# Transposing a 4096 x 4096 adjacency: by DMA from a bf16 copy in DRAM, in place of TensorE's products with the identity

## The chip, the cores and the metric

The kernel runs on one core of a Trainium2 chip. The metric is the time of one execution on the device, in microseconds, as the median of several runs. A profile is one further execution with the hardware profiler on.

## What is computed

The input is x (4096 nodes x 512) and a 0/1 adjacency of 4096 x 4096 in float32. Two graph layers follow each other, each with a residual and a layer normalisation:

```python
# layer 0: graph attention, 4 heads of 128
support = (x @ weight).reshape(N, 4, 128)
logits  = f1[j] + f2[i]              # of support, per head
w       = leaky_relu(logits, 0.2) * adjacency[i, j]
attn    = softmax over j of w where it is not 0
out     = attn @ support + bias + x @ proj_w + proj_b
x1      = layernorm(x + out)
# layer 1: masked attention, 8 heads of 64
adj     = max(adjacency, eye)
scores  = q @ k.T / 8 + 0.01 * eye - 1e16 * (1 - adj)
out     = layernorm(x1 + softmax(scores) @ v @ Wo)
```

Both layers sum over the neighbours j of a node i, and both put j on the partitions, since the products over j contract along the partitions. So both need the adjacency with j on the partitions and i along the free dimension, which is the transpose of the order in which it lies in DRAM.

## The kernel before, in words

The function is `tile_gat_then_masked_attention` (from line 430). The order of the instructions on each engine is that of the program text, so where a call stands decides what waits behind it in a queue. The stages:

1. **Layer-0 projections** (lines 569 to 675, 0 to 285 us). Eight groups g of 512 rows, four tiles of 128 rows each. TensorE transposes x (line 634) and multiplies by the two weights (lines 647 and 651); VectorE makes f1 and f2, GpSimd scales support (line 606), SP stores base (line 667), support (line 611) and the row factors (line 619) to DRAM.
2. **Layer-0 attention** (lines 683 to 802, 316 to 1314 us). Four windows w of 1024 nodes i, four heads h in each, 32 blocks j of 128 neighbours: 512 steps. A step makes z on ScalarE (line 712), masks it with the transposed adjacency on VectorE (line 715, one for two steps), forms p (line 719), and eight products on TensorE add into o_ps (line 793). `front` runs LA = 3 steps ahead of the products. After a window's last head, ScalarE divides, GpSimd adds base by an accumulating DMA (line 752), and the normalised rows are stored (line 762) and transposed for layer 1.
3. **Layer-1 projections** (lines 808 to 858): q, k and v to DRAM.
4. **Layer-1 attention** (lines 860 to 1067, from 1693 us). Eight groups g of 512 nodes, four pairs of heads m, 32 blocks j: 1024 units, three to a step. Scores on TensorE (line 933), exponential on ScalarE (line 942), mask on VectorE (line 948), sums on GpSimd (line 956), products on TensorE (line 966). The four blocks on the diagonal use md, a float32 copy of their part of the adjacency to which VectorE adds the diagonal (line 889). `loads` (line 901) fetches k and v one chunk of eight units ahead, the next group's adjacency during m = 3, and md during m = 1.

**The adjacency's way.** `load_rows` (line 536) has GpSimd load 1024 rows x 512 columns from DRAM and narrow them to bf16 on the way, into one of two buffers `arow`. `transpose_adj` (line 543) makes eight 128 x 128 transposes of one block j of a window (line 553, into PSUM), ScalarE copies them to `stage` (line 560), and SP stores two blocks at a time to the DRAM tensor `adjT_d` (line 562). Window 0 is made during the layer-0 projections, one block per tile of 128 rows and two more; windows 1 to 3 during layer-0 attention of the window before, one block every third step while u = 32h + j is below 96. `load_adjT0` (line 565) loads a tile of 128 x 4 x 1024 bf16 (1 MB) of it for layer 0, into 9 buffers of which a window uses 8; the loads of the next window are issued during head 3. In layer 1, `load_adjT` (line 876) loads 128 x 8 x 512 (1 MB) and `load_md` (line 880) has GpSimd load 128 x 4 x 512 and widen it to float32 on the way.

Of the kernel before, what the change touches and what calls it, by code (L numbers as in the profile page):

```python
# [429 lines left out]
def tile_gat_then_masked_attention(  # L430
# [46 lines left out]
    ident_b = const.tile([P, P], BF16, name="ident_b")  # L477
    make_identity(nc, ident_b)
# [19 lines left out]
    adjT_d = [dram.tile([P, NT, W], BF16, name=f"adjT_d{w}") for w in range(NW)]  # L498
# [28 lines left out]
    with tc.tile_pool(name="l0", bufs=1) as l0, \  # L527
            tc.tile_pool(name="l0a", bufs=2) as rows_p, \
# [5 lines left out]
        arow, stage, adjT = {}, {}, {}  # L534

        def load_rows(w, c):
            arow[w, c] = rows_p.tile([P, WT, CJ * P], BF16, name="arow")
            nc.gpsimd.dma_start(  # L538
                arow[w, c],
                adj[w * W:(w + 1) * W, c * CJ * P:(c + 1) * CJ * P].rearrange(  # L540
                    "(t p) n -> p t n", p=P))

        def transpose_adj(w, j, ps):


            c = j // CJ
            if j % CJ == 0:
                nxt = (w, c + 1) if c + 1 < NCJ else (w + 1, 0)
                if nxt[0] < NW:
                    load_rows(*nxt)  # L550
            p = ps.tile([P, WT, P], BF16, name="at_ps", bufs=1)
            for t in range(WT):
                nc.tensor.transpose(p[:, t, :], arow[w, c][:, t, j % CJ * P:(j % CJ + 1) * P],  # L553
                                    ident_b)

            def go():
                if j % 2 == 0:
                    stage[w, j // 2] = rows_p.tile([P, 2, W], BF16, name="stage")
                s = stage[w, j // 2]
                nc.scalar.activation(s[:, j % 2, :], p.rearrange("p t r -> p (t r)"), AF.Copy)  # L560
                if j % 2:
                    nc.sync.dma_start(adjT_d[w][:, j - 1:j + 1, :], s)
            return go

        def load_adjT0(w, c):
            adjT[w, c] = adjT_p.tile([P, CJ, W], BF16, name="adjT")
            nc.sync.dma_start(adjT[w, c], adjT_d[w][:, c * CJ:(c + 1) * CJ, :])

        with tc.tile_pool(name="l0s", bufs=2) as sp, \
# [19 lines left out]
            load_rows(0, 0)  # L589
# [34 lines left out]
            blocks = list(range(NT))  # L624
            loaded = 0
            for g in range(NG):
# [56 lines left out]
        with tc.tile_pool(name="l0w", bufs=2) as wp, \  # L683
# [16 lines left out]
            def front(w, h, j):  # L700
                n = w * H0 + h
                if n == 0 and j == 0:
                    load_pass(w, h)
                if j == 2 * LA and n + 1 < len(passes):
                    load_pass(*passes[n + 1])
                if h == H0 - 1 and w + 1 < NW and j % CJ == 2:
                    load_adjT0(w + 1, j // CJ)
                fr = fr_t[w, h]
                if j % 2 == 0:
                    z = wp.tile([P, 2, W], BF16, name="z")  # L710
                    for k in range(2):
                        nc.scalar.activation(z[:, k, :], fr[:, 0, :], AF.Abs,  # L712
                                             bias=f1s[:, j + k, h:h + 1], scale=BIG)
                    az = wp.tile([P, 2, W], BF16, name="az")
                    nc.vector.tensor_tensor(az, adjT[w, j // CJ][:, j % CJ:j % CJ + 2, :], z,  # L715
                                            op=ALU.min)
                    az_t[w, h, j // 2] = az
                p = wp.tile([P, W], F32, name="p", bufs=LA + 1)
                nc.vector.scalar_tensor_tensor(p, fr[:, 1, :], dj[:, j, h:h + 1],  # L719
                                               az_t[w, h, j // 2][:, j % 2, :],  # L720
                                               op0=ALU.max, op1=ALU.mult)
                p_t[w, h, j] = p
# [57 lines left out]
            for n, (w, h, j) in enumerate(steps):  # L780
# [16 lines left out]
                if take:  # L797
                    later.at(2, take)
# [6 lines left out]
    with tc.tile_pool(name="l1", bufs=1) as l1:  # L805
# [54 lines left out]
        with tc.tile_pool(name="l1w", bufs=2) as wp, \  # L860
# [11 lines left out]
            def of_group(g, j0, j1):  # L872
                r = g * G % W
                return adjT_d[g * G // W][:, j0:j1, r:r + G]

            def load_adjT(g, c):
                at[g, c] = wp.tile([P, CH, G], BF16, name="adjT1", bufs=NCH + 2)
                nc.sync.dma_start(at[g, c], of_group(g, c * CH, (c + 1) * CH))

            def load_md(g):  # L880

                md = wp.tile([P, GT, G], F32, name="md")
                nc.gpsimd.dma_start(md, of_group(g, g * GT, (g + 1) * GT))  # L883
                mdt[g] = md
# [236 lines left out]
```

## Time and profile before

| | |
|---|---|
| median of three runs | 3914.03 us (3912.95 to 3914.14) |
| profiled execution's own time | 3914.05 us |
| its span | 3912.2 us |
| mean granted TensorE clock | 0.985 |
| TensorE busy | 3780.8 us, 97% |
| VectorE busy | 2536.0 us, 65% |
| GpSimd busy | 2055.2 us, 53% |
| ScalarE busy | 1858.0 us, 47% |
| DMA, mean of the 16 engines | 447.47 MB, 114 GB/s |

The span runs from the first to the last instruction; 1.85 us of the profiled execution lie outside it. A group's row gives the source line, the engine, what it writes and reads, the shape and count, and after the bar its busy time and the mean duration of one in ns, then the idle time of the engine just before these instructions and what ended most of it. A float32 product counts as two instructions on TensorE. Slices are fortieths of the span, 98 us each. SPq, POOLq and ACTq are the queues from which SyncE, GpSimd and ScalarE issue DMAs.

### The profile page before, as it was taken

The page shows a single profiled execution, that of the slowest core. Times are in us where ns is not written, and L with a number is a line of the kernel's source. Part 1 is how long each engine was busy: PE and PEld are TensorE (multiplying, and loading weights), DVE is VectorE, ACT ScalarE, POOL GpSimd, SP SyncE. Part 2 cuts the span into 40 slices and gives each one's busy share as a digit, 9 for nine tenths or more (in the row PEclk, how much of TensorE's full clock was granted, in tenths as well). Part 3 has the DMA queues.
Part 4 walks back from the last instruction along what each step waited for, and adds up shares of the span by engine and source line. Part 5 has one row for each costly group of instructions (what it writes and reads, how often), then busy time and mean ns, then how long its engine had stood idle before and what let it go on. Part 6 is the DMA issues. An engine that isn't in the chain of part 4 may idle for free. (4 is left out here: it accounts for less than half of the span.)

```text
span 3912.2 us, 51842 instructions
## 1 busy us (share of the span) xinstructions
PE 3780.8 (97%) x20490; PEld 1971.1 (50%) x20490; DVE 2536.0 (65%) x2432; ACT 1858.0 (47%) x2113; POOL 2055.2 (53%) x1211
## 2 busy tenths in 40 slices
PE   7987999999999699989999999999999999999998
PEld 3447999999999544433333333333333333333332
DVE  3447999999999400036666666666666666666665
ACT  1226767777666300034554444444444444444443
POOL 2320013030030200048888888888888888888886
PEclk9998999999999799999999999999999999999999
DMA  6885657666430422342322322323223223223211
GB/s 163 195 197 151 148 195 174 193 175 155 171 95 34 135 100 89 108 145 76 116 81 77 112 87 70 116 81 106 91 81 122 64 87 113 89 86 103 78 63 51
DMA packets 232429, 447.47 MB, mean 114 GB/s; under 512 B 21744, under 2 KB 136688, under 8 KB 225008
## 3 DMA queue, kind: packets, MB, share of 16 engines
q1 hardware_dynamic: 179264, 386.38, 29.9%
q0 software_dynamic: 42432, 51.39, 8.0%
q10 hardware_dynamic: 10480, 6.29, 0.5%
q8 instruction: 163, 2.67, 0.3%
q14 instruction: 90, 0.74, 0.1%
HBM read 372.51 MB, written 100.86 MB: 121 GB/s over the span
## 5 line engine op out<-in xcount | busy, mean ns | idle before, releaser
L956 POOL TENSOR_TENSOR q_sum<-q_sum,p 128x1024 f32<-128x1024 f32 x704 | 1660.1, 2358 | 331.7 <-DVE p L948 286.3
L948 DVE TENSOR_TENSOR p<-s_ps,adjT 128x1024 f32<-128x1024 f32 x896 | 1044.4, 1218 | 685.6 <-ACT s_ps L942 668.8
L942 ACT ACTIVATE s_ps<-s_ps 128x1024 f32<-128x1024 f32 x1024 | 971.2, 1008 | 1002.3 <-PE s_ps L933 1001.9
L933 PE MATMUL s_ps<-q_sb,k_sb 64*128 64x512 f32 x4096 | 980.9, 610 | 16.4 <-issue 10.1
L793 PE MATMUL o_ps<-sup_t,p 128*128 128x129 f32 x8192 | 951.6, 277 | 37.9 <-DVE p L719 37.8
L966 PE MATMUL o_ps<-p,v_sb 128*64 128x512 f32 x4096 | 956.3, 601 | 0.0
L793 PEld LDWEIGHTS o_ps<-sup_t,p 128*128 128x128 f32 x8192 | 929.7, 192 | 46.1 <-issue 29.4
L933 PEld LDWEIGHTS s_ps<-q_sb,k_sb 64*128 64x128 f32 x4096 | 367.1, 187 | 627.9 <-issue 388.7
L719 DVE SCALAR_TENSOR_TENSOR p<-fr_t,dj,az 128x1024 f32<-128x1024 f32 x512 | 638.8, 1282 | 34.1 <-PE o_ps L793 6.7
L712 ACT ACTIVATE z<-fr_t,f1s 128x1024 bf16<-128x1024 f32 x512 | 556.2, 1141 | 144.7 <-DVE az L715 118.4
L966 PEld LDWEIGHTS o_ps<-p,v_sb 128*64 128x64 f32 x4096 | 263.0, 136 | 649.9 <-issue 621.5
L715 DVE TENSOR_TENSOR az<-adjT,z 128x2048 bf16<-128x2048 bf16 x256 | 311.7, 1218 | 26.6 <-ACT z L712 26.5
L752 POOL DMA_DIRECT2D agg<-base_d x32 | 29.3, 1046 | 447.8 <-ACT agg L740 446.6
L538 POOL DMA_DIRECT2D arow<-in_adj_dram x32 | 29.9, 933 | 423.1 <-PE at_ps L553 423.1
L560 ACT ACTIVATE stage<-at_ps 128x1024 bf16<-128x1024 bf16 x128 | 130.9, 1023 | 199.8 <-PE at_ps L553 195.5
L948 DVE TENSOR_TENSOR p<-s_ps,md 128x1024 f32<-128x1024 f32 x128 | 150.5, 1218 | 94.6 <-ACT s_ps L942 93.4
L883 POOL DMA_DIRECT2D md<-adjT_d x8 | 6.6, 825 | 353.0 <-DMA v_d<-vg 352.7
L837 DVE COPY kg<-k_ps 128x512 f32<-128x512 f32 x32 | 22.1, 691 | 194.7 <-PE k_ps L834 194.7
L977 PE MATMUL sm_ps<-p,ones 128*32 128x512 f32 x1024 | 136.4, 605 | 0.0
L844 ACT ACTIVATE qg<-q_ps 128x512 f32<-128x512 f32 x32 | 19.1, 598 | 236.3 <-PE q_ps L841 236.3
L661 DVE TENSOR_TENSOR prod<-sup,uv 128x512 f32<-128x512 f32 x64 | 51.8, 809 | 116.7 <-ACT sup L657 116.7
L834 PE MATMUL k_ps<-xT,wk 128*128 128x512 f32 x256 | 116.9, 600 | 10.4 <-DMA xT<-x1T_d 10.4
(89 smaller groups left out, 2111.3 us busy)
## 6 DMA issues: line engine op xcount, KB each, us to landing
adjT<-adjT_d SPq DMA_DIRECT2D x64, 1024.0 KB, 7.5
k_sb<-k_d SPq DMA_DIRECT2D x128, 512.0 KB, 3.5
v_sb<-v_d SPq DMA_DIRECT2D x128, 512.0 KB, 3.5
sup_t<-sup_d SPq DMA_DIRECT2D x16, 2064.0 KB, 13.0
arow<-in_adj_dram POOLq DMA_DIRECT2D x32, 1024.0 KB, 12.4
adjT_d<-stage SPq DMA_DIRECT2D x64, 512.0 KB, 5.3
fr_t<-fr_d SPq DMA_DIRECT2D x16, 1024.0 KB, 8.9
sup_d<-sup SPq DMA_DIRECT2D x32, 258.0 KB, 10.7
```

Source lines behind the costliest of these rows:

```text
L560: nc.scalar.activation(s[:, j % 2, :], p.rearrange("p t r -> p (t r)"), AF.Copy)
L712: nc.scalar.activation(z[:, k, :], fr[:, 0, :], AF.Abs, bias=f1s[:, j + k, h:h + 1], scale=BIG)
L715: nc.vector.tensor_tensor(az, adjT[w, j // CJ][:, j % CJ:j % CJ + 2, :], z, op=ALU.min)
L719: nc.vector.scalar_tensor_tensor(p, fr[:, 1, :], dj[:, j, h:h + 1], az_t[w, h, j // 2][:, j % 2, :], op0=ALU.max, op1=ALU.mult)
L793: nc.tensor.matmul(o[t // BK][:, t % BK, :], p[:, t * P:(t + 1) * P], sup_t[w, h][:, j, :], start=(j == 0 and t % BK == 0), stop=(j == NT ...
L834: nc.tensor.matmul(k_ps, w3["wk"][:, c, m * P:(m + 1) * P], xT[:, c, :], start=(c == 0), stop=(c == KC - 1))
L933: nc.tensor.matmul(s[:, e, :], k[r, a:a + P], qt[g, m][r, :], start=True, stop=True)
L942: nc.scalar.activation(s, s, AF.Exp)
L948: nc.vector.tensor_tensor(p, s, mask.to_broadcast([P, HP, G]), op=ALU.mult)
L956: nc.gpsimd.tensor_tensor(q_sum[g, m], q_sum[g, m], p, op=ALU.add)
L966: nc.tensor.matmul(o[r, :], v[:, j % CH, r], p[:, e, :], start=(j == 0), stop=(j == NT - 1))
L977: nc.tensor.matmul(sm_t[g, m][r:r + QD, :], ones[:, 0:QD], pt[g, m, j - 1 + n][:, e, :], start=(j == 3), stop=(j + 6 >= BY_PE))
```

## The change

The narrowed adjacency is no longer loaded into SBUF. `narrow(w, c)` has GpSimd copy 1024 rows x 512 columns from DRAM to DRAM, to bf16 on the way; `adj_d[w][c]` keeps it. SP's transposing DMA then brings it into the same tiles as before: 32 of 1 MB for layer 0, and for layer 1, where a tile spans two of the copies, 64 of half a megabyte. For md, SP transposes half a megabyte into a bf16 tile `mdb`, of one buffer, and GpSimd's DMA widens it from there into md (8 times). All transposes on TensorE of the adjacency, ScalarE's copies of them, the stores to `adjT_d` and the tiles `arow`, `stage` and `ident_b` are gone. The first two narrowing copies are issued at the start, the others of window 0 one every four tiles of rows, two ahead; those of a later window every 16 steps of the window before.

In the program that this gives, GpSimd's queue has the eight narrowing copies of window 1 directly behind its last scaling of support (none of them waits for a buffer), and in windows 1 and 2 the first copy of the window after stands behind the second accumulating load of base. On SP, the layer-1 attention begins with q, k and v of the first chunk, two transposes of the first tile, that of mdb, the six others of the group, and then k and v of the second chunk.

```diff
-    ident_b = const.tile([P, P], BF16, name="ident_b")
-    make_identity(nc, ident_b)
-    adjT_d = [dram.tile([P, NT, W], BF16, name=f"adjT_d{w}") for w in range(NW)]
+    adj_d = [[dram.tile([W, CJ * P], BF16, name=f"adj_d{w}_{c}") for c in range(NCJ)]
+             for w in range(NW)]
...
-        def load_rows(w, c):
-            arow[w, c] = rows_p.tile([P, WT, CJ * P], BF16, name="arow")
-            nc.gpsimd.dma_start(
-                arow[w, c],
-                adj[w * W:(w + 1) * W, c * CJ * P:(c + 1) * CJ * P].rearrange(
-                    "(t p) n -> p t n", p=P))
-
-        def transpose_adj(w, j, ps):
...
+        def narrow(w, c):
+            nc.gpsimd.dma_start(adj_d[w][c],
+                                adj[w * W:(w + 1) * W, c * CJ * P:(c + 1) * CJ * P])
 
         def load_adjT0(w, c):
             adjT[w, c] = adjT_p.tile([P, CJ, W], BF16, name="adjT")
-            nc.sync.dma_start(adjT[w, c], adjT_d[w][:, c * CJ:(c + 1) * CJ, :])
+            nc.sync.dma_start_transpose(adjT[w, c], adj_d[w][c])
...
-            load_rows(0, 0)
+            narrow(0, 0)
+            narrow(0, 1)
...
                     i = g * GT + t
-                    take = transpose_adj(0, blocks.pop(0), ps) if i >= 2 else None
+                    if i % CJ == 0 and i // CJ + 2 < NCJ:
+                        narrow(0, i // CJ + 2)
...
-                    if take:
-                        take()
-                    if i in (NT // 3, 2 * NT // 3):
-                        transpose_adj(0, blocks.pop(0), ps)()
...
                     if i % CJ == CJ - 1:
-                        ready = (NT - len(blocks)) // CJ
-                        while loaded < ready:
-                            load_adjT0(0, loaded)
-                            loaded += 1
+                        load_adjT0(0, i // CJ)
...
+                if w + 1 < NW and (h * NT + j) % (H0 * CJ) == 2 * CJ:
+                    narrow(w + 1, (h * NT + j) // (H0 * CJ))
                 if h == H0 - 1 and w + 1 < NW and j % CJ == 2:
                     load_adjT0(w + 1, j // CJ)
...
-                take = None
-                u = h * NT + j
-                if w + 1 < NW and u % 3 == 0 and u // 3 < NT:
-                    take = transpose_adj(w + 1, u // 3, ps)
...
-                if take:
-                    later.at(2, take)
...
-            def of_group(g, j0, j1):
+            def turn_in(dst, g, j0):
                 r = g * G % W
-                return adjT_d[g * G // W][:, j0:j1, r:r + G]
+                nc.sync.dma_start_transpose(dst, adj_d[g * G // W][j0 // CJ][r:r + G, :])
 
             def load_adjT(g, c):
                 at[g, c] = wp.tile([P, CH, G], BF16, name="adjT1", bufs=NCH + 2)
-                nc.sync.dma_start(at[g, c], of_group(g, c * CH, (c + 1) * CH))
+                for n in range(0, CH, CJ):
+                    turn_in(at[g, c][:, n:n + CJ, :], g, c * CH + n)
 
             def load_md(g):
-                md = wp.tile([P, GT, G], F32, name="md")
-                nc.gpsimd.dma_start(md, of_group(g, g * GT, (g + 1) * GT))
-                mdt[g] = md
+                mdb = wp.tile([P, GT, G], BF16, name="mdb", bufs=1)
+                turn_in(mdb, g, g * GT)
+                mdt[g] = wp.tile([P, GT, G], F32, name="md")
+                nc.gpsimd.dma_start(mdt[g], mdb)
```

More of the change, by code (lines that the diff above doesn't have):

```diff
@@ L527, in tile_gat_then_masked_attention @@
     with tc.tile_pool(name="l0", bufs=1) as l0, \
-            tc.tile_pool(name="l0a", bufs=2) as rows_p, \
             tc.tile_pool(name="l0t", bufs=NCJ + 1) as adjT_p:
@@ L533, in tile_gat_then_masked_attention @@
         dj = l0.tile([P, NT, H0], F32, name="dj")
-        arow, stage, adjT = {}, {}, {}
-        def load_rows(w, c):
-            arow[w, c] = rows_p.tile([P, WT, CJ * P], BF16, name="arow")
-            nc.gpsimd.dma_start(
-                arow[w, c],
-                adj[w * W:(w + 1) * W, c * CJ * P:(c + 1) * CJ * P].rearrange(
-                    "(t p) n -> p t n", p=P))
-        def transpose_adj(w, j, ps):
[L546 to L563, printed above, removed]
+        adjT = {}
+        def narrow(w, c):
+            nc.gpsimd.dma_start(adj_d[w][c],
+                                adj[w * W:(w + 1) * W, c * CJ * P:(c + 1) * CJ * P])
         def load_adjT0(w, c):
             adjT[w, c] = adjT_p.tile([P, CJ, W], BF16, name="adjT")
-            nc.sync.dma_start(adjT[w, c], adjT_d[w][:, c * CJ:(c + 1) * CJ, :])
+            nc.sync.dma_start_transpose(adjT[w, c], adj_d[w][c])
         with tc.tile_pool(name="l0s", bufs=2) as sp, \
@@ L622, in factors @@
                 later.at(3, rest)
-            blocks = list(range(NT))
-            loaded = 0
             for g in range(NG):
```

## Prediction

> **What bounds the kernel now.** I read the page from the top: the busy shares, then the slices, to find the stages.
>
> ```profile
> span 3912.2 us, 51842 instructions
> ...
> PE   7987999999999699989999999999999999999998
> ...
> DVE  3447999999999400036666666666666666666665
> ...
> DMA  6885657666430422342322322323223223223211
> ```
>
> One slice is 98 us. TensorE is full nearly everywhere; the dips are the start, the seam between the layer-0 projections and layer-0 attention (315 us) and the seam into layer-1 attention (1690 us). VectorE is as full as TensorE in layer-0 attention (slices 4 to 13) and nowhere else. From 1700 us on TensorE alone bounds, and no transpose of the adjacency runs there, so the change acts before that point or at the seams. The groups, shapes apart, price the removed work:
>
> ```profile
> L793 PE MATMUL o_ps<-sup_t,p 128*128 128x129 f32 x8192 | 951.6, 277 | 37.9 <-DVE p L719 37.8
> L719 DVE SCALAR_TENSOR_TENSOR p<-fr_t,dj,az 128x1024 f32<-128x1024 f32 x512 | 638.8, 1282 | 34.1 <-PE o_ps L793 6.7 <-DVE az L715 0.9
> L715 DVE TENSOR_TENSOR az<-adjT,z 128x2048 bf16<-128x2048 bf16 x256 | 311.7, 1218 | 26.6 <-ACT z L712 26.5
> L560 ACT ACTIVATE stage<-at_ps 128x1024 bf16<-128x1024 bf16 x128 | 130.9, 1023 | 199.8 <-PE at_ps L553 195.5 <-DMA adjT_d<-stage 4.1 <-ACT sup L657 0.3
> L553 PE MATMUL at_ps<-ident_b,arow 128*128 128x128 bf16 x1024 | 78.0, 219 | 3.0 <-ACT stage L560 2.1 <-DVE fr_row L617 0.9
> ```
>
> TensorE gives the transposes 78 us, 2% of the span. That is no gain yet: in layer-0 attention VectorE needs 1282 + 1218/2 = 1891 ns per step (one of 512), and TensorE 951.6/512 = 1.86 us without transposes. The busy time by stretches, of line 793 alone, shows who leads where (16 rows of this line are one step):
>
> ```profile
> 380.00:500.00 120.00, 114.05 (x983) 1.00 0.57 142
> 506.00:556.00 50.00, 50.00 (x450) 1.00 0.66 238
> 1140.00:1190.00 50.00, 49.93 (x430) 1.00 0.02 9
> ```
>
> With transposes a step takes 120 x 16/983 = 1.953 us; without them, after TensorE has fallen behind and VectorE has work stored up, 50 x 16/450 = 1.778; in window 3, which never has transposes, 50 x 16/430 = 1.860, VectorE's pace. So window 3 is already what the other windows can become. The same view of everything gives the seams:
>
> ```profile
> 40.00:285.00 245.00, 239.19 (x858) 117.41 (x857) 122.72 (x181) 64.01 (x108) 74.81 (x94) 1.00 0.83 183
> 285.00:315.70 30.70, 0.61 (x9) 0.47 (x8) 4.13 (x10) 4.93 (x5) 3.80 (x7) 0.55 0.87 232
> 1690.00:1703.00 13.00, 4.40 (x12) 1.83 (x12) 0.45 (x3) 2.61 (x3) 0.77 (x1) 0.61 1.01 317
> ```
>
> The columns are TensorE, weight loads, VectorE, ScalarE and GpSimd busy, then granted clock, DMA share, GB/s. In both seams TensorE is idle and the DMA engines are full: there the transfers set the time. The timeline says which ones:
>
> ```profile
> 285.49 0.37 SPq L567 DMA_DIRECT2D adjT<-adjT_d  x1
> 287.86 0.94 POOL L538 DMA_DIRECT2D arow<-in_adj_dram  x1
> 287.94 2.27 SPq L611 DMA_DIRECT2D sup_d<-sup  x4
> 304.33 0.36 SPq L693 DMA_DIRECT2D fr_t<-fr_d  x1
> ...
> 1693.57 0.77 POOL L883 DMA_DIRECT2D md<-adjT_d  x1 [352.69 <-DMA v_d<-vg]
> 1694.40 9.63 SPq L878 DMA_DIRECT2D adjT<-adjT_d  x4
> 1702.55 0.90 DVE L889 TENSOR_TENSOR md<-md,ident_e 128x128 f32<-128x128 f32 x4 [14.11 <-ACT s_ps L942]
> ```
>
> **What the Trainium skill says.** "DMA: Bandwidth & Descriptors", Latency and other measured facts, gives a transposing DMA 261 GB/s with a non-contiguous middle dimension, which is the form here: 1.05 MB in 4.0 us. No run here shows one yet. "VectorE: DVE Perf Modes", The three transpose paths, gives 1309 ns for one 128x128 block by DMA and 390 by TensorE; the trace has eight TensorE transposes in 0.61 us, 76 ns each, so these are prices of one alone; 32 of them per MB, 41.9 us, is the upper end. Queues, rings and completion order, on the first page, says a DMA engine goes round robin between the queues packet by packet; the trace agrees as far as it can, since the seam's transfers of both queues end together (below). DMA Transpose (X-bar), same page, says only SP and ScalarE may issue one; the changed program has all 104 on SP.
>
> **The price of a transpose, T (1 MB).** The trace has no such DMA. Nearest: the weights read in 256-byte rows (queue q10, 1335 to 1700 us), 8192 packets of 18 ns each. A megabyte is 4096 of them: 4096 x 18 / 16 engines = 4.6 us. Ends: 4.0 and 41.9 us. I take T = 5 us.
>
> **The change, part by part** (on the profiled run: span 3912.2, its own time 3914.05, the median 3914.03, so sums on the span carry over with 1.85 us outside it).
>
> *Layer-0 projections (to 285 us): gain 13.6.* The timeline has a block of eight transposes start at 47.77 and the product behind it at 48.21: 0.44 us on TensorE's path, which is 239 of 245 us busy there. 31 blocks lie before TensorE's end: -13.6. ScalarE's 1.02 us copies go too, but ScalarE is busy 64 of 245: nothing. The DMA share is 0.83, so what goes and comes must balance: by packet records the stores of line 562 (2048 x 167 ns) and the loads of line 567 (1024 x 396 ns) hold 21.4 + 25.3 = 46.7 us of all 16 engines; eight transposes cost 8T = 40. The narrowing DMA has the packets of the old row load (1 KB written, 105 ns). Balanced at T = 5; if they came to more than the 42 us idle there, the gain would go back.
>
> *Start: loss 3.4.* Two narrowing DMAs are issued ahead of the first group, where one row load was. VectorE's first add waits for bb (22.6 us), and its copies of xT stand behind it in its queue, so TensorE waits too. The weights take 96 packets per engine of 90 ns, x 64 of 104, one row load 64 of 105: 22 us, as seen. In turns, the second one puts up to 32 more ahead: 32 x 105 = 3.4. Bounds 0 and 6.7.
>
> *First seam: loss 10.3.* In the old order GpSimd's row loads wait for the two arow buffers (46 us until 335 us); a narrowing DMA has no buffer to wait for, and after its last sup product GpSimd issues all eight of window 1 at some 0.93 us each, from 288 us. SP's fr_t load waits until sup_d's stores have landed. Before: adjT 3.2 (8 x 396 ns) + sup_d 9.0 (128 x 70 ns) + arow 6.7 = 18.9 us from 285.5, which is the 304.3 observed. After: T + 9.0 + one narrowing packet per sup_d packet, 128 x 105 = 13.4: 27.4, +8.6; the fr_t load that follows shares its 16 packets in the same way, +1.7. Bounds: +1.9 (only one narrowing DMA gets in) and +20.
>
> *Layer-0 attention: gain 8.* Windows take 246.1, 250.8, 252.9 and 248.4 us. Window 0 becomes 128 x 1.860 + 4 for its start and the closing work of passes = 242 (-4); windows 1 and 2 do what window 3 does, 248.4 (-2.4, -4.5): -10.9. VectorE is next in line and takes the rest of the 0.49 us that a block cost. ScalarE's copies again give nothing. In windows 1 and 2 one narrowing DMA now stands among the base loads of the normalisation in GpSimd's queue; VectorE's statistics wait for those: +1.5 each. SP holds eight transposes while VectorE frees the adjT buffers; the last is needed about 108 us after the first is issued, so they cost nothing up to T = 108/8 = 13.5. Sum -8, bounds -11 and +2.
>
> *Layer-1 start: loss 7.3.* The first mask needs md. Then: issued at 1693.6, landed for VectorE at 1702.5. Now it is the third half-size transpose on SP, then a GpSimd cast that waits for its landing: 1694.4 + 1.5T + 2 (landing, as k_d's stores) + 0.8 (issue) + 5.1 (median landing of the old one) = 1709.8 at T = 5, +7.3. Behind it queue six more halves, and behind those k and v of the second chunk: there at 1694.4 + 4.5T + 3.5 (median landing of k) = 1720.4; TensorE wanted them 11 us after the first product of the mask (1714.3 before), now 1721.6: just in time.
>
> *Layer-1 steady state: 0.* SP issues loads up to a chunk (17 us) ahead, limited by the three k and v buffers; per group nine halves, 4.5T = 22 of 273 us, at a DMA share of 0.2 to 0.3. GpSimd's queue holds the md cast, with the q_sum adds behind it, and VectorE's p behind those; the cover is SP's lead and 10 p buffers. Without it each of seven groups would lose T/2 + 2, some 30 us in all.
>
> Sum: -13.6 + 3.4 + 10.3 - 8 + 7.3 = -0.6, so 3913.4 us: a removed 78 us that buys nothing.
>
> **The rivals.**
> *Gain kept* (12%): the narrowing DMAs don't crowd the first seam (+1.9 there, 0 at the start). -13.6 + 1.9 - 10.9 + 7.3 = -15: 3899. For it: TensorE is full in the projections. Against: GpSimd has nothing else to do there.
> *Layer-1 start waits for transposes* (25%, the other side): T between 6 and 13.5. It decides from T = 6, where both md and the second k chunk are late. At 8: seam +13.3, md +11.8, k at 1733.9 against 1726.1, +7.8; -13.6 + 3.4 + 13.3 - 8 + 19.6 = +14.7: 3929. At 13.5: seam +18.8, md +20, k +24, the projections' gain halved: -6.8 + 3.4 + 18.8 - 8 + 44 = +51, 3965. For it: these are many small rows on full queues.
> *Transposes pace layer 0* (18%): T above 13.5. At 20: 8 x 6.5 = 52 us in each of three windows, 75 at the layer-1 start, projections bound by DMA: about 4170. For it: the 1309 ns; against: the 261 GB/s and the 18 ns packets.
> That the change doesn't do what it says isn't open: the program has no transpose of the adjacency on TensorE.
>
> **How the numbers follow.** The forecast (T from 4 to 6, 45%) lies within 3900 to 3922. A difference under about 0.2% (7.8 us) can't be told from none here: faster means below 3906.2, slower above 3921.9. Faster: 15 from the forecast, 11 from the first rival: 26%. Same: 27 + 1 + 4 = 32%. Slower: 3 + 21 + 18 = 42%. Range 3900 to 3985: below it lie some 7%, above it 13% of the last rival.
>
> **What would show it.** T is read from the landing of the transposes; steps of windows 0 to 2 at 1.86 us throughout; projection steps 0.44 us shorter; fr_t issued some 27 us after SP's last transpose of the projections, where 18.8 us lay (285.49 to 304.33); first masked product of layer 1 near 1710 less what was won before. Wrong if T is far from 5, if SP itself is busy for microseconds per transpose, or if GpSimd waits for mdb within the groups.

## The result, and the profile after

The change makes no difference that this measurement can tell: 3913.12 us median (3911.36 to 3920.28) where the kernel before takes 3913.66 (3912.95 to 3914.14); ratio of their means 1.0002, 95% interval 0.9985 to 1.002. The profiled execution took 3912.06 us, with a span of 3910.3. The prediction said 3913.4. Its sum is right by luck: as the tables below show, the terms of the sum are too small on both sides, by about as much.

The page of the kernel after, the same rows as were shown of before:

```profile
span 3910.3 us, 49558 instructions
...
PE   7977999999999699979999999999999999999998
...
DMA  7976177474520523252422422423324224223211
...
L758 PE MATMUL o_ps<-sup_t,p 128*128 128x129 f32 x8192 | 956.2, 278 | 65.3 <-DMA sup_t<-sup_d 46.3
```

TensorE's transposes (78.0 us) and ScalarE's copies of them (130.9 us) are gone, and the span is 1.9 us shorter. The row of line 758 (793 before) tells where one part went: the idle time ahead of it grew from 37.9 to 65.3 us, and its largest part is no longer VectorE's p but one wait of 46.3 us for a DMA, the load of sup_t. That is the first seam.

The busy time by stretches (TensorE, weight loads, VectorE, ScalarE, GpSimd, then granted clock, DMA share, GB/s) of everything, in the two seams of the kernel after:

```profile
270.00:300.00 30.00, 0.00 (x0) 0.00 (x0) 0.00 (x0) 0.00 (x0) 7.25 (x12) 0.54 1.25 193
1681.00:1703.00 22.00, 5.77 (x14) 2.51 (x16) 2.97 (x6) 3.02 (x3) 0.57 (x1) 0.58 1.11 275
```

The projections end 16.6 us earlier, at 267.6 instead of 284.3 us, and then 30 us pass in which no engine but GpSimd does anything (its 7.25 us are the issues of its copies and its last scaling). In both seams the DMA engines are full, as they were before (the share adds up the times of packets, which can overlap, so it can pass 1). To see what each stage gave I took the stages' borders from the trace: first product of the projections (line 621, 647 before), their last product (625, 651), first attention product (758, 793), its last, first and last product of the layer-1 projections (797 to 813), first scores of group 1. In us, the forecast's terms beside the differences:

| stretch | before | after | difference | forecast |
|---|---|---|---|---|
| start to first product | 24.9 | 27.1 | +2.2 | +3.4 |
| layer-0 projections | 259.4 | 240.5 | -18.9 | -13.6 |
| first seam | 31.4 | 47.0 | +15.6 | +10.3 |
| layer-0 attention | 998.2 | 984.2 | -14.0 | -8 |
| to layer-1 projections, and these | 373.8 | 375.8 | +2.0 | 0 |
| end of these to group 1 | 275.9 | 286.3 | +10.4 | +7.3 |
| groups 1 to 7 and the end | 1948.5 | 1949.3 | +0.8 | 0 |

So 33 us are won where TensorE and VectorE bound the time, and 28 us are lost at the start and in the two seams, where transfers do. The 2.8 us of the two rows that the forecast left at nothing are within what such rows differ by from run to run (below); no loss is hidden in the long layer-1 part.

The first seam in the timeline of the kernel after (start, length in us, engine or queue, line, what it does; in brackets the idle time before and what ended it):

```profile
268.87 4.73 SPq L541 DMA_TRANSPOSE adjT<-adj_d  x1
...
271.24 6.01 POOL L536 DMA_DIRECT2D adj_d<-in_adj_dram  x8
273.70 4.31 SPq L586 DMA_DIRECT2D sup_d<-sup  x4
...
298.79 0.36 SPq L660 DMA_DIRECT2D fr_t<-fr_d  x1
299.21 0.46 SPq L665 DMA_DIRECT2D sup_t<-sup_d  x1
...
309.00 6.34 ACT L681 ACTIVATE z<-fr_t,f1s 128x1024 bf16<-128x1024 f32 x6 [40.95 <-DMA fr_t<-fr_d]
...
314.66 1.63 PE L758 MATMUL o_ps<-sup_t,p 128*128 128x129 f32 x6 [46.27 <-DMA sup_t<-sup_d]
```

Four delays follow each other. SP itself is busy for 4.73 us with issuing one transpose (before, 0.37 us for the load in its place), so the stores of sup_d are issued at 273.70, 2.4 us after GpSimd had finished sup (271.31). The eight narrowing copies enter right then. The load fr_t, which waits for the stores, is issued 29.9 us after the transpose (18.8 before), lands 10.2 us later (6.3 before), and sup_t, asked for at 299.21, is the last to come.

The layer-1 start of the kernel after, in the same view:

```profile
1681.40 6.23 SPq L838 DMA_TRANSPOSE adjT<-adj_d  x2
...
1687.67 2.08 SPq L838 DMA_TRANSPOSE mdb<-adj_d  x1
...
1689.79 15.87 SPq L838 DMA_TRANSPOSE adjT<-adj_d  x6
1692.98 0.57 POOL L850 DMA_DIRECT2D md<-mdb  x1 [367.25 <-DMA mdb<-adj_d]
1700.03 0.90 DVE L855 TENSOR_TENSOR md<-md,ident_e 128x128 f32<-128x128 f32 x4 [24.59 <-DMA adjT<-adj_d]
```

Nine half-size transposes hold SP from 1681.40 to 1705.66, 2.7 us each. VectorE's wait is put down to a landing of adjT, but what its instruction needs is md: cast by the DMA that GpSimd issued at 1692.98, after mdb had landed; this cast landed at 1699.46.

### The profile page after: what moved, and what is told of

It reads as the page before. It is cut to its first block, busy times and chain, and to the rows that moved or that the text cites. A ratio compares the mean times of both kernels' runs of the same rounds, so it can differ in the third digit from the quotient of the medians.

```text
span 3910.3 us, 49558 instructions
## 1 busy us (share of the span) xinstructions
PE 3743.3 (96%) x19466; PEld 1922.6 (49%) x19466; DVE 2528.4 (65%) x2432; ACT 1743.3 (45%) x1985; POOL 2052.7 (52%) x1209
## 5 line engine op out<-in xcount | busy, mean ns | idle before, releaser
L922 POOL TENSOR_TENSOR q_sum<-q_sum,p 128x1024 f32<-128x1024 f32 x704 | 1659.9, 2358 | 332.3 <-DVE p L914 287.0
L758 PE MATMUL o_ps<-sup_t,p 128*128 128x129 f32 x8192 | 956.2, 278 | 65.3 <-DMA sup_t<-sup_d 46.3
L899 PE MATMUL s_ps<-q_sb,k_sb 64*128 64x512 f32 x4096 | 981.9, 610 | 25.7 <-DVE p L914 15.4
L684 DVE TENSOR_TENSOR az<-adjT,z 128x2048 bf16<-128x2048 bf16 x256 | 311.5, 1217 | 41.6 <-ACT z L681 41.4
L972 PE MATMUL s_ps<-wo_sb,on 128*128 128x512 f32 x256 | 120.7, 616 | 4.2 <-POOL on L968 4.2
L807 ACT ACTIVATE qg<-q_ps 128x512 f32<-128x512 f32 x32 | 19.1, 597 | 236.7 <-PE q_ps L804 236.7
L581 POOL TENSOR_TENSOR sup<-sup,aj 128x512 f32<-128x512 f32 x32 | 33.5, 1046 | 160.9 <-issue 118.6
L621 PE MATMUL s_ps<-w_sb,xT 128*128 128x512 f32 x256 | 116.7, 599 | 0.0
## 6 DMA issues: line engine op xcount, KB each, us to landing
adj_d<-in_adj_dram POOLq DMA_DIRECT2D x32, 1024.0 KB, 26.2
```

The lines of the kernel that those rows point to most:

```text
L758: nc.tensor.matmul(o[t // BK][:, t % BK, :], p[:, t * P:(t + 1) * P], sup_t[w, h][:, j, :], start=(j == 0 and t % BK == 0), stop=(j == NT ...
L899: nc.tensor.matmul(s[:, e, :], k[r, a:a + P], qt[g, m][r, :], start=True, stop=True)
L922: nc.gpsimd.tensor_tensor(q_sum[g, m], q_sum[g, m], p, op=ALU.add)
L972: nc.tensor.matmul(s, on_t[g][:, m, t * P:(t + 1) * P], wo_sb[:, m, :], start=(m == 0), stop=(m == NP1 - 1))
```

## The experiments

My theory after the comparison: the removed transposes were worth about 30 us of the span, and the change gives them back in two places that have little to do with transposing itself: a burst of eight narrowing copies in the first seam, which nothing holds back any more, and SP's queue at the layer-1 start, in which nine transposes stand ahead of what is needed first. The rival: the transposing DMAs are dear by themselves (SP's time, the queues' time), and would cost the same wherever they stood.

The stretches of each run, in us, as in the table above (the gap is that before the layer-1 projections, which are left out: 331 to 333 in all):

| kernel | start | projections | seam | attention | gap | to group 1 | span |
|---|---|---|---|---|---|---|---|
| before | 24.9 | 259.4 | 31.4 | 998.2 | 42.2 | 275.9 | 3912.2 |
| after | 27.1 | 240.5 | 47.0 | 984.2 | 43.1 | 286.3 | 3910.3 |
| copies held back | 28.2 | 240.1 | 27.6 | 984.6 | 41.6 | 287.0 | 3890.2 |
| last transpose later | 28.4 | 242.0 | 42.8 | 983.7 | 42.4 | 286.5 | 3907.9 |
| md first | 28.9 | 245.2 | 47.6 | 984.0 | 42.4 | 291.4 | 3920.7 |
| early md and first tile | 28.8 | 241.5 | 48.8 | 983.8 | 45.1 | 281.5 | 3910.6 |
| the same, k and v first | 29.3 | 243.9 | 47.2 | 984.0 | 44.9 | 274.8 | 3905.5 |
| transposed twice | 28.8 | 241.1 | 47.3 | 991.8 | 41.1 | 286.8 | 3916.9 |
| before, row load held | 25.7 | 259.5 | 25.7 | 999.3 | 41.5 | 276.2 | 3910.0 |
| combined | 27.0 | 244.2 | 28.2 | 984.6 | 45.1 | 272.9 | 3884.1 |
| combined, again | 26.0 | 241.2 | 27.5 | 985.0 | 44.6 | 272.3 | 3876.6 |
| before, repaired | 25.8 | 258.9 | 26.5 | 997.2 | 46.7 | 272.2 | 3908.0 |

What a stretch that an edit doesn't touch differs by from run to run is the grain of this table: up to 5 us in the projections (240.1 to 245.2), 1 to 2 in the attention and in the seam (47.0 to 48.8), 2 at the start. One execution of each was profiled; those of "md first" (3922.49 us) and of "the same, k and v first" (3907.38) were the slowest of theirs, 6.1 and 4.5 us above the median, so a few us between two rows say little alone.

### 1. The narrowing copies of window 1 held back

```diff
                 if w + 1 < NW and (h * NT + j) % (H0 * CJ) == 2 * CJ:
+                    if w == 0:
+                        nc.gpsimd.tensor_copy(tick, az_t[w, h, j // 2 - 1][:, 0, 0:1])
                     narrow(w + 1, (h * NT + j) // (H0 * CJ))
```

The copy of one column into `tick` makes GpSimd wait until the mask product of a step has run; each narrowing copy stands behind its own.

> The changed kernel, with each of window 1's eight narrowing copies held until the layer-0 attention has made a mask product: GpSimd first copies one element of az. Theory (the eight copies issued at once fill the DMA queues just when sup_d, fr_t and sup_t have to pass): the stretch from TensorE's last projection to its first attention product falls from 47.0 us to 30 to 36, and the time by 11 to 17 us, to 3896 to 3902. Rival (the transposing DMA ahead of sup_d on SP is what delays it): the stretch stays above 42 us and the time within 5 us of the changed kernel's.

Measured: 3893.73 us (3891.97 to 3899.96) against 3916.33 of before; ratio 0.9945, interval 0.9931 to 0.9958. The seam takes 27.6 us, 19.4 less than after:

```profile
274.13 2.52 SPq L586 DMA_DIRECT2D sup_d<-sup  x4
...
284.72 0.36 SPq L661 DMA_DIRECT2D fr_t<-fr_d  x1
...
295.94 20.25 PE L761 MATMUL o_ps<-sup_t,p 128*128 128x129 f32 x162 [26.89 <-DVE p L691]
```

SP still needs 4.5 us for its transpose and sup_d is still issued at 274.1, but fr_t follows 10.6 us later instead of 25.1 and lands in 6.2 us, and the first narrowing copy is issued at 306.8. By the packet records the 2048 packets of sup_d go out within 7.8 us; in the kernel after it takes 19.1 us, with some 2390 packets of the narrowing copies between them. TensorE's first product no longer waits for sup_t but for p, so for the first steps of the pipeline itself. So the burst costs 19.4 us here, more than the forecast and this theory had given it, and more than the whole loss of 15.6: without it the seam is even 3.8 us shorter than before.

### 2. The last transpose of window 0 issued after the seam's loads

```diff
-                    if i % CJ == CJ - 1:
+                    if i % CJ == CJ - 1 and i < NT - 1:
                         load_adjT0(0, i // CJ)
...
             load_pass(0, 0)
+            load_adjT0(0, NCJ - 1)
```

> The changed kernel, with the last transpose of window 0 issued after the first pass's loads instead of ahead of sup_d's stores; the eight narrowing copies stay where they are. Rival (the transpose ahead of sup_d delays the seam): SP is free 2.5 us earlier and 5 us of transpose packets are out of the way, so the stretch falls by 5 to 7.5 us, to about 40 us. Theory (the narrowing copies share every packet's turn): sup_d starts 2.5 us earlier but still takes turns with the copies, so 2 to 4 us are won and the stretch stays above 43.

Measured: 3914.32 us, ratio 0.9993 (0.9986 to 0.9999). sup_d is issued as soon as GpSimd has finished sup (274.01 and 274.03 us; 271.31 and 273.70 in the kernel after). The seam is 42.8 us, 4.2 less than after: between the two, just past the theory's 2 to 4 us and short of the rival's 5 to 7.5. So the transpose at this place costs about its own time on SP, and not several times that; with the burst in, the seam stays at 43. What it costs once the burst is out was not run: no kernel here has both edits.

### 3. md transposed ahead of the first tile

```diff
                     load_kv(0, 0, 0)
-                    load_adjT(0, 0)
                     load_md(0)
+                    load_adjT(0, 0)
                     for c in range(1, NCH):
```

> The changed kernel, with md's transpose ahead of the first tile's two at the start of layer-1 attention. Theory (the first masked product waits for three half transposes one after the other and then for the widening copy): md is there two halves earlier, so the stretch from TensorE's last layer-1 projection to the first masked product falls from 26.2 us by 5 to 6.5, to about 20, and the time by as much. Rival (the widening copy shares the queues with the other transposes and lands last anyway): under 2 us.

Measured: 3916.41 us, ratio 1.0 (0.9992 to 1.0008). My theory fell. The first masked product comes 23.4 us after the end of the layer-1 projections (26.15 in the kernel after), a gain of 2.7, and group 1 starts 5.1 us later:

```profile
1686.36 5.50 SPq L838 DMA_TRANSPOSE mdb<-adj_d  x1
1691.90 20.99 SPq L838 DMA_TRANSPOSE adjT<-adj_d  x8
...
1712.93 0.58 SPq L859 DMA_DIRECT2D k_sb<-k_d  x1
...
1717.41 2.08 PE L899 MATMUL s_ps<-q_sb,k_sb 64*128 64x512 f32 x4 [2.83 <-DMA k_sb<-k_d]
1719.42 4.86 PE L932 MATMUL o_ps<-p,v_sb 128*64 128x512 f32 x12
```

Being first brings md little: its transpose takes SP 5.50 us there (2.08 as the third), its cast, issued at 1695.18, is there for VectorE at 1702.32, after 7.1 us among eight other transposes. And the wait then moves on: k of the second chunk is issued behind all nine (1712.93), and TensorE waits for it. That wait is 2.83 us, but it costs more: the four products behind it take 2.08 us and the twelve after them 4.86, where the same groups take 1.13 and 2.80 at full clock; the granted clock from 1717 to 1721 us is 0.50. Between the projections and group 1 TensorE is idle for 26.4 us (25.7 in the kernel after) and busy for 265.1 (260.6), so most of the 5.1 us are products at the lower clock. The order among the nine matters less than their number ahead of k; experiments 4 and 5 test that.

### 4. md and the first tile transposed during the layer-1 projections

```diff
+        def turn_first(g):
+            if g == 2:
+                turn_in(mdb0, 0, 0)
+                nc.gpsimd.dma_start(md0, mdb0)
+            if 3 <= g < 3 + len(at0):
+                c = g - 3
+                for n in range(0, CH, CJ):
+                    turn_in(at0[c][:, n:n + CJ, :], 0, c * CH + n)
...
-                at[g, c] = wp.tile([P, CH, G], BF16, name="adjT1", bufs=NCH + 2)
+                at[g, c] = wp.tile([P, CH, G], BF16, name="adjT1", bufs=NCH + 1)
...
-                    load_adjT(0, 0)
-                    load_md(0)
-                    for c in range(1, NCH):
-                        load_adjT(0, c)
+                    mdt[0] = md0
+                    for c in range(NCH):
+                        if c < len(at0):
+                            at[0, c] = at0[c]
+                        else:
+                            load_adjT(0, c)
```

> The changed kernel, with the first group's md and first tile transposed during the layer-1 projections, into buffers of their own (one adjT1 buffer fewer, to make room). Theory (the layer-1 start is all waiting for transposes): the first masked product follows the first exponential, so the stretch falls from 26.2 us to 13 to 15 and the time by 11 to 13 us, to 3900 to 3902. Rival (q, k and v queue behind or the second chunk of k and v comes late behind the six other halves, so TensorE waits there instead): under 6 us are won. If the smaller number of adjT1 buffers costs anything, groups 1 to 7 get longer than 273.4 us each.

Measured: 3912.82 us, ratio 0.9991 (0.9985 to 0.9998). Both are right in part. The first masked product comes 13.8 us after the projections, as the theory has it; but the stretch to group 1 only falls by 4.8 us, to 281.5, since the next wait takes over:

```profile
1686.84 16.88 SPq L776 DMA_TRANSPOSE adjT<-adj_d  x6
...
1703.77 0.58 SPq L871 DMA_DIRECT2D k_sb<-k_d  x1
...
1709.65 2.08 PE L913 MATMUL s_ps<-q_sb,k_sb 64*128 64x512 f32 x4 [5.82 <-DMA k_sb<-k_d]
```

Six transposes that nobody needs for another 17 us hold SP for 16.88 us, and k of the second chunk stands behind them. The buffer given up costs nothing: groups 1 to 7 and the end take 1949.6 us (1949.3). The early tiles do cost something elsewhere: in the four kernels that have them (experiments 4, 5, 8 and 10) the gap ahead of the layer-1 projections is 44.6 to 45.1 us, where the other versions of the kernel after have 41.1 to 43.1, and TensorE waits there for the load of wk and no longer for xT. Why wk comes later was not followed up.

### 5. The same, with k and v of the second chunk ahead of the six

```diff
                     mdt[0] = md0
+                    load_kv(0, 0, 1)
                     for c in range(NCH):
```

> The kernel of the early first tile (e4), with k and v of the second chunk issued ahead of the six other half transposes. Theory (what is left at the layer-1 start is that k and v stand behind the halves on SP): TensorE's wait of 5.8 us for k goes, the stretch from the last layer-1 projection to the first scores of group 1 falls from 281.4 us to 274 to 277, and the time by 4 to 7 us against e4. Rival (the halves' total transfer is the limit, and the second tile's masks come late instead): at most 2 us.

Measured: 3902.87 us, ratio 0.9968 (0.9957 to 0.998). The stretch is 274.8 us: the theory's, 6.7 less than in experiment 4 and 11.5 less than in the kernel after. So the loss at the layer-1 start lay in what stands ahead on SP's queue, in two places one behind the other: ahead of md, and then ahead of k.

### 6. Each later transpose of layer 0 issued twice

```diff
             nc.sync.dma_start_transpose(adjT[w, c], adj_d[w][c])
+            if w:
+                again = adjT_p.tile([P, CJ, W], BF16, name="again", bufs=2)
+                nc.sync.dma_start_transpose(again, adj_d[w][c])
```

> The changed kernel, with every transposing DMA of windows 1 to 3 issued twice in layer 0, the second time into a tile that nobody reads (24 more transposes of 1 MB; only work is added). Forecast's cover (free up to 13.5 us per MB; two take some 10 to 11): windows 1 to 3 stay at 247.7, 248.2 and 248.6 us within 1 us and the time within 4 us of the changed kernel's. Rival (SP or the queues are nearly full there): a window gets longer by 24 us or more, 8 tiles of some 3 us over VectorE's pace.

Measured: 3922.07 us, ratio 1.0021 (1.0013 to 1.0029). The attention takes 991.8 us, 7.6 more; windows 0 to 3 take 239.8, 251.5, 251.9 and 248.6 (after: 239.7, 247.7, 248.2, 248.6). Neither was right: 24 more transposes, over 100 us of SP's time at 4.2 us each, are not free, but no window loses more than 3.8 us, where the rival asks 24. All of it lies in the first pass (head) of windows 1 and 2, where the window before is normalised: 71.5 and 71.9 us where after has 67.7 and 68.2. The trace lists for the DMA that adds base (line 721, in this kernel 724) what waited for it, with us and times; in the kernel after, and then in this one:

```profile
  DVE bn_st L512: 11.9, 6
```

```profile
  DVE bn_st L512: 19.3, 9
```

VectorE's statistics wait 7.4 us longer for base, which is the 7.6 (the longest of these loads lands after 20.1 us, 12.3 in the kernel after). The steps of the attention themselves don't wait for any transpose. The extra transposes slow those loads but are not enough alone: window 3 starts with just as many of them and loses nothing, and there the longest load of base lands after 14.0 us (6.7 in the kernel after) and nobody waits for it. What windows 1 and 2 have besides is a narrowing copy of the next window among the loads of base. So it takes both together, as far as this one run shows. With the single transposes of the kernel after, the wait is what it was in the kernel before (12.2 us).

### 7. The kernel before, with its first free row load held

```diff
+                if (w, j) == (1, 0):
+                    nc.gpsimd.tensor_copy(tick, held[0][:, 0, 0:1])
                 if nxt[0] < NW:
                     load_rows(*nxt)
```

> The kernel before the change, with the one row load that falls into the first seam (the second of window 1) held until a mask product has been made. It tells how much of e1's gain the old kernel could have had. Theory: sup_d without a row load beside it lands in some 10.6 us as in e1, so fr_t is issued 5 to 7 us earlier, the stretch falls from 31.4 us to 24 to 26.5 and the time by 5 to 7 us. Rival (nothing else in that stretch depends on the row load): unchanged within 2 us.

Measured: 3910.58 us, ratio 0.9988 (0.9981 to 0.9994); seam 25.7 us, as the theory has it. So even the one row load that the kernel before let into its seam cost 5.7 us there. With no row load and no narrowing copy in it, the seam takes 25.7 and 26.5 us in the kernel before (experiments 7 and 9) and 27.5 to 28.2 in the kernel after (1, 8 and 10), where the transpose still stands ahead of sup_d.

### 8. The repairs together

Experiments 1 and 5, and the second narrowing copy of the start issued in the first tile instead of ahead of it:

```diff
             narrow(0, 0)
-            narrow(0, 1)
...
+                    if i == 0:
+                        narrow(0, 1)
                     if i % CJ == 0 and i // CJ + 2 < NCJ:
```

> The changed kernel with all three repairs: narrowing copies of window 1 held (e1), first tile and md early with k and v of the second chunk first (e5), and one narrowing copy at the start in place of two (the second follows the first group's sums). Theory: 19.4 from the seam, 11 from the layer-1 start and 2 to 3 from the start add up, since they lie one after another on TensorE's path: 3880 to 3884 beside a kernel before of 3914. Rival (what is won in one seam is lost in the next, as the copies now fall into the attention or the transposes into the projections): above 3890.

Measured: 3885.13 us, ratio 0.9919 (0.9906 to 0.9932), against 3915.75 of before on the same chip: it beats the kernel before clearly, and so, by 0.8%, the kernel after, which was level with that (they were not run side by side). The theory's 3880 to 3884 was for a before of 3914. The seam takes 28.2 us, the stretch to group 1 272.9. The start, 27.0, is hardly repaired.

### 9 and 10. The kernel before with the same repairs, and the combined version again

Would the kernel before gain as much from the repairs? It gets the held row load of experiment 7, md and the first tile loaded during the layer-1 projections, and k and v of the second chunk ahead of the other tiles:

```diff
+        def load_first(g):
+            if g == 2:
+                nc.gpsimd.dma_start(md0, adjT_d[0][:, 0:GT, 0:G])
+            if g == 3:
+                nc.sync.dma_start(at0, adjT_d[0][:, 0:CH, 0:G])
```

> The kernel before, with the repairs of the combined version made to it as far as it has the same places: the row load that its first attention step released early is held until a mask product has run (as in the earlier run of the kernel before), and md and the first adjacency tile of layer 1 are loaded during the layer-1 projections, with k and v of the second chunk ahead of the other three tiles. Theory (the repairs belong to the seams, and the transposes on TensorE cost the projections and the attention some 15 to 19 and 14 us of their own): seam 1 stays at 25 to 27, the stretch from the layer-1 projections to the scores of group 1 falls from 276 to 272 to 274, projections (259 to 260) and attention (998 to 1000) stay: 6 to 9 us below the kernel before, and 22 to 28 us above the combined version. Rival (most of the combined version's lead is repair that the kernel before could have had as well): 15 us or more below the kernel before, less than 15 above the combined version.

> The combined version once more, beside the repaired kernel before on the same chip. Theory: 0.991 to 0.9935 of the kernel before, as in its first run (0.9919), with stretches of 27 to 29 (seam 1), 984 to 985 (attention) and 272 to 275 us (to the scores of group 1). Rival: the first run was a good one, and the ratio is above 0.994.

Measured, against 3915.56 of before: the repaired kernel before 3909.93 us, ratio 0.9985 (0.9978 to 0.9992); the combined version 3880.74, ratio 0.991 (0.9894 to 0.9925). The combined version comes out as in its first run. The rival of experiment 9 falls: before gains only 5.6 us from its repairs, a little under the 6 to 9 that I gave it, and the combined version stands 29.2 us below it, a little over the 22 to 28. 3.7 us to group 1 are won, but the gap ahead of the layer-1 projections grew by 4.5. The trace shows where: GpSimd issues the early load of md at 1335.07, inside that gap, and ScalarE then waits 5.65 and 4.51 us for the last stores of x1T (3.56 and 2.37 before). If the one causes the other, which wasn't tested, this repair is not as good as it could be, and with md loaded later before might come some 4 us lower; the rival would still fall. Their seams (26.5 and 27.5) and starts of layer 1 (272.2 and 272.3) are alike; they differ in the projections (258.9 and 241.2) and in layer-0 attention (997.2 and 985.0), 29.9 us together. That is what it was worth to take 78 us of transposes off TensorE, with the copies and stores that went with them; with md loaded later in before, it might be a few us less.

## Why the prediction was right, step by step

The conclusion held: a removed 78 us that buys nothing, since the seams give it back. The sum came out within 0.3 us of the median, but none of its four large terms was hit within 3 us; gains of 21.6 were 32.9, losses of 21.0 were 28.2 and 2.8 of small change. Two errors of some 10 us cancel, so the mechanism was right and the closeness of the number is luck. In the order of its steps:

*Layer-0 projections, -13.6, measured -18.9.* The mechanism was right, the count was short. The kernel before, where an extra block is made, and then the kernel after:

```profile
113.78 0.61 PE L553 MATMUL at_ps<-ident_b,arow 128*128 128x128 bf16 x8 [1.00 <-ACT stage L560]
114.23 3.65 PE L647 MATMUL s_ps<-w_sb,xT 128*128 128x512 f32 x8
117.72 3.60 PE L651 MATMUL b_ps<-pw_sb,xT 128*128 128x512 f32 x8
```

```profile
119.12 3.60 PE L621 MATMUL s_ps<-w_sb,xT 128*128 128x512 f32 x8
122.56 3.60 PE L625 MATMUL b_ps<-pw_sb,xT 128*128 128x512 f32 x8
```

The product behind a block takes 3.49 us to the next start (114.23 to 117.72), and 3.44 without one (119.12 to 122.56): the products behind a block are slower, too, 30 x 0.055 = 1.7. The two extra blocks wait for ScalarE's copy, 1.00 us and more of an idle TensorE, since at_ps has one buffer: 1.16 + 1.28 = 2.4. And 32 blocks x 0.446 = 14.3, where the forecast counted 31. Together 18.4. (Over the nine runs that have these projections the mean is 242.2 us, over the three of the kernel before 259.3: -17.1, so some of it is taken back in other runs.) "ScalarE is busy 64 of 245: nothing" is the step that failed, by these 2.4 us: an engine with time to spare can still be waited for.

*Start, +3.4, measured +2.2.* Right in kind: VectorE's first add of bb starts at 24.83 us instead of 22.61. The combined version, with the second copy issued later, is at 27.0 and 26.0, where the others that start like the kernel after have 27.1 to 29.3: 1 to 2 us may be had back that way, which is what the start differs by from run to run.

*First seam, +10.3, measured +15.6: the largest loss, mis-sized.* "One narrowing packet per sup_d packet" was nearly right: some 2390 came on 2048. The Trainium skill (DMA: Bandwidth & Descriptors, Queues, rings and completion order) says that an engine goes round robin between its queues and drains a whole packet, typically 9 to 17 descriptors, before it turns to the next. The trace's 1.17 to 1 agrees with equal turns in the mean; its records don't name the engine, so neither the order nor the length of a turn is shown. The rest of the term was off piece by piece. From SP's transpose to the first packet of sup_d 8.6 us pass (277.5), where the sum had T = 5: SP's 4.73 us of issuing, and then 3.8 us from the stores' issue to their first packet. In experiment 1 these are 1.2 us, so most of that is the burst's, too. The stores' stretch is 19.1 us and not 22.4. fr_t follows 2.2 us behind the last packet, which the sum didn't have. That makes 29.9 us instead of 27.4. fr_t's landing is 3.9 us longer than before (10.2 and 6.3), and not 1.7, and sup_t, last at 314.66, adds the remaining 0.6: 11.1 + 3.9 + 0.6 = 15.6. Experiments 1 and 2 part it by cause: 19.4 us go when the copies are held, 4.2 when the transpose is moved. Together that is more than 15.6, since the seam of before held a row load of its own, worth 5.7 (experiment 7), and the two gains need not add.

*Layer-0 attention, -8, measured -14.0.* The steps do what was forecast. TensorE's busy time of line 758 in windows 0, 1 and 3 of the kernel after (16 rows are one step):

```profile
318.00:368.00 50.00, 50.00 (x440) 0.98 0.52 109
640.00:690.00 50.00, 49.35 (x425) 1.00 0.70 147
1140.00:1190.00 50.00, 49.35 (x427) 1.00 0.17 65
```

Window 1 now runs as window 3, at VectorE's pace, and window 2 does the same (425 rows in 900 to 950 us). But that pace was misread. The 1.860 us of the prediction came from a stretch in which TensorE was busy for 49.93 of 50 us, so it is TensorE's own pace with work stored up; the prediction's sum for VectorE had given 1.891. Later in window 3 of the kernel before, TensorE has caught up and waits:

```profile
1200.00:1250.00 50.00, 49.35 (x425) 1.00 0.01 2
```

That is 1.882 us a step, as in the kernel after. Three of the six us that were missed are the "+1.5 each" for the narrowing copies among the loads of base: VectorE's wait for base is 11.9 us (12.2 before), so the cover held. Window 0 became 239.7 and not 242: the 4 us for its start and closing work are not there, 128 steps of 1.884 us (the mean of its last two passes) are already 241.1. The first steps are short, as VectorE has worked ahead while sup_t was late (440 rows in the first 50 us, 1.82 us a step); that brings back little of the seam's loss, since window 0 takes 240.2 in experiment 1, where sup_t isn't late.

*Layer-1 start, +7.3, measured +10.4.* Each term was a little short: three halves took SP 8.3 us (1.5T = 7.5), landing to issue 3.2 (2), the cast 7.1 to VectorE's start (5.9). k of the second chunk came in time in the kernel after, as forecast; experiments 3 and 4 show that it is next in line as soon as md is earlier.

*Steady state, 0, measured +0.8.* SP's lead covers it; GpSimd waits for mdb once, at the start (367.25 us there, which is the idle time since layer 0).

*T = 5 us per MB.* All rivals that rested on T above 6 fall. By the packet records one MB is 4096 packets of 256 bytes at 20 to 21 ns, 5.3 us of all 16 engines, and those of the last transpose of window 0 pass within 4.85 us (270.28 to 275.13); the 261 GB/s of the Trainium skill (DMA: Bandwidth & Descriptors, Latency and other measured facts) would be 4.0, so the measured rate is about four fifths of it. The prediction wanted to read T from the landing: that is 6.6 us after the issue, which would be the second rival's range. But 1.4 us of it lie ahead of the first packet, and transposes that stand one behind the other follow at a shorter distance: 2.7 us for half a MB at the layer-1 start. The second rival's sign, k of the second chunk late, is absent in the kernel after. The prediction named "SP itself is busy for microseconds per transpose" as what would make it wrong. It is:

```profile
L541 SPq DMA_TRANSPOSE adjT<-adj_d x32: 3874/4202/10687, 57.5 to 1037.7; - x32
```

The three figures are the least, the median and the longest in ns: 4.2 us in the median, nearly T itself. It did no harm to the sum because T was taken as serial on SP's queue anyway; it did harm where something else stood behind on SP, in both seams.

*Gain kept*, 15 us, did not happen, and was too low for what the change can be worth: with the seams repaired in both kernels it is some 29.

## What to carry to other kernels

When a buffer goes, the wait for it goes too: look for what that wait was holding back, and at whose transfers it will now push in; a wait of one small instruction on GpSimd was worth 19 us here. A change that moves work from a bound engine to a queue is paid at the seams, so size each seam by the whole chain that is queued behind the new entry, to the last load that the next stage needs, and not to the first. A sum that comes out right shows little by itself; check its terms stage by stage.

## What the runs showed that I had not expected

- A transposing DMA holds SP for nearly as long as it takes to move the data: 4.2 us per MB, where the plain load of the same tile held it 0.32 us. In experiment 2, issued behind the burst, it held SP 27.72 us; why so long isn't settled.
- A copy from DRAM to DRAM that narrows 1 MB lands after 8.3 to 65.6 us (median 26.2), longest where eight are queued together; the row loads into SBUF, which two buffers held apart, took 8.9 to 23.9 (median 12.4).
- A group of eight float32 products directly behind eight bf16 transposes is busy 0.05 us longer than one without (3.65 and 3.60 us).
- A wait of TensorE cost more than its own length: close behind those of 2.83 and 5.82 us for k (experiments 3 and 4) twelve products took 4.86 and 3.59 us instead of 2.80.
